# A 17-tap convolution by nested Toom-Cook products over groups of four batches

## The chip, the cores and the metric

The kernel runs on one core of a Trainium2 chip. The metric is the device time of that core in microseconds (us). A core has a matrix engine (TensorE, PE in the profile, its weight loads as PEld), three engines for elementwise work (VectorE or DVE, ScalarE or ACT, GpSimd or POOL) and a queue, SyncE or SP, that issues the DMA transfers. Each engine takes its own instructions in the order of the program and waits on the others by semaphores.

## The reference

For 32 batches of 512 tokens with 256 channels (B = 32, N = 512, D = 256), all in float32:

```python
h = jnp.maximum(_layernorm(x, axis=-1), 0.0)
xc = jnp.transpose(h, (0, 2, 1))
c = relu(bn1(conv1d(xc, conv1_w, pad=0)))                 # one tap
c = bn2(conv1d(c, conv2_w, pad=8))                        # 17 taps, 256 -> 256 channels
x_conv = jnp.transpose(relu(c + xc), (0, 2, 1))
s = h @ w_se.T + b_se                                     # three coordinates
A = jnp.exp(-squared_distance(s, s)) * adj
x_nmp = A @ relu(h @ w_msg.T + b_msg)
gi = jnp.concatenate([x_conv, x_nmp], axis=-1) @ w_ih.T + b_ih
gh = h @ w_hh.T + b_hh
r, z = sigmoid(gi_r + gh_r), sigmoid(gi_z + gh_z)
n = jnp.tanh(gi_n + r * gh_n)
out = x + (1 - z) * n + z * h
```

## The kernel before

One batch is worked after the other. Channels lie on the 128 partitions (two chunks of 128, ND = 2) and the 512 tokens on the free dimension; the layer norm, the messages and the residual have tokens on partitions (four chunks, NT = 4). Each output of 128 channels by 512 tokens fills one PSUM bank; there are five banks for sums (`ps_acc`) and three for transposes and positions (`ps_tr`). `matmul_sum` (L68) issues nearly all matrix multiplications, so its line holds many stages and they are told apart by the names of their tiles. A float32 multiplication is two MATMUL records in the trace, a float32 transpose is one.

The stages of a batch, each a function:
- `load`, `load_adj` (L75, L79): DMA of `x` (512 KB) and of the mask (1 MB).
- `norm` (L160 to L166): statistics on DVE, the power -1/2 on POOL (L119), scaling on DVE.
- `norm_t` (L177, L178): eight transposes, then ReLU on ACT gives `hT`.
- `conv1` (L185): the one-tap convolution; ACT writes it into `h1`, which has 8 zeros at both ends of the tokens.
- `positions` (L194 to L197): the two factors `left` and `right` of the distances.
- `messages` (L209, L210), `kernel_exp` (L218, L220), `masked` (L231, L232), `gather` (L253).
- `conv2` (L243, L246): for each half of the output channels one sum of 17 taps by two input chunks, 34 multiplications of 512 columns; a tap is a shifted slice of `h1`.
- `gates` (L276 to L298): three gates for each half of the channels, on TensorE, ACT, DVE and POOL.
- `finish` (L307 to L312): transposes back, residual, output DMA.

The program order is written out by hand (`manual_schedule`), so a buffer that is to be used again makes its next user wait. In that order batch b's `conv1`, `positions`, `messages` and `kernel_exp` come first, then `finish` of batch b - 1, `norm` of b + 1, the first half of `conv2`, `masked`, the second half of `conv2`, `norm_t` of b + 1, `gather` and `gates`. All weights of the 17 taps (`w2`) stay in SBUF.

## Time and profile before

| what | value |
|---|---|
| device time, median of 3 runs | 3608.95 us (3608.85 to 3609.02) |
| span of the profiled execution | 3607.8 us |
| granted TensorE clock, mean | 0.999 |
| TensorE busy | 3585.4 us |
| DVE, ACT, POOL busy | 506.7, 493.6, 281.3 us |
| `conv2` multiplications (`ps_acc<-h,w`) | 4352 records, 1878.8 us busy |
| DMA over the span | 76.00 MB, mean 21 GB/s |

The span runs from the first to the last instruction of one profiled execution; 1.15 us lie between it and the median of the runs. Busy time is the union of an engine's instructions; matrix multiplications are pipelined, so the price of one in a row of them is the distance between starts, not its own duration. In a group of the profile stand the line, the engine, the operation, output and inputs by tile name, shapes and count, then busy time, mean duration of one in ns, and the idle time of the engine just before them with what ended it. The chain that ended last goes back from the last instruction to whatever released it.

### The profile page before, as it was taken

How to read it: one execution, taken by the hardware profiler on the slowest of the kernel's cores; microseconds unless marked ns; L12 is line 12 of the kernel's file. 1: busy time of each engine (PE TensorE's matmuls, PEld its weight loads, DVE VectorE, ACT ScalarE, POOL GpSimd, SP SyncE). 2: the span in 40 equal slices, each digit the busy share in tenths (PEclk: the TensorE clock that was granted, in tenths of full speed). 3: DMA queues.
4: the chain of work that ended last, by engine and by line, in shares of the span. 5: the costliest groups of instructions: out<-in, count | busy, mean ns of one | idle time of the engine just before them, and what ended most of it. 6: DMA issues, size and time to landing. Idle time of an engine off the chain costs nothing.

```text
span 3607.8 us, 21656 instructions
## 1 busy us (share of the span) xinstructions
PE 3585.4 (99%) x9344; PEld 1678.9 (47%) x9344; DVE 506.7 (14%) x1006; ACT 493.6 (14%) x704; POOL 281.3 (8%) x241
## 2 busy tenths in 40 slices
PE   9999999999999999999999999999999999999998
PEld 4444444444444444444444444444444444444444
DVE  1111111111111101111011110111101111111111
ACT  1111011110111101111011110111111111111110
POOL 0000000000000000000000000000000000000000
PEclk9999999999999999999999999999999999999999
DMA  3000000000000000000000000000000000000000
GB/s 136 24 12 12 24 24 24 12 17 19 24 24 12 24 12 24 24 12 24 12 24 24 12 24 12 24 23 22 14 12 24 24 24 12 12 24 24 6 6 6
DMA packets 53858, 76.00 MB, mean 21 GB/s; under 512 B 3202, under 2 KB 36098, under 8 KB 53634
## 3 DMA queue, kind: packets, MB, share of 16 engines
q1 hardware_dynamic: 53762, 74.61, 6.3%
q8 instruction: 73, 1.20, 0.1%
q14 instruction: 23, 0.19, 0.0%
HBM read 57.83 MB, written 16.78 MB: 21 GB/s over the span
## 4 chain that ended last, share of the span: by engine, by line
PE 98%; DVE 1%; issue 0%; DMA 0%; POOL 0%; POOLq 0%; ACT 0%; ACTq 0%; DVEq 0%
PE ps_acc L68 91%; PE ps_acc L218 3%; PE ps_tr L68 2%; PE ps_tr L177 1%; PE ps_tr L307 1%; DVE at L232 1%; PE ps_tr L231 1%; DVE conv_t L243 0%; DMA x_sb<-in_x_dram 0%; DVE st L160 0%; POOLq L389 0%; POOL gate_t L296 0%; POOL gate_t L297 0%; POOL rstd L119 0%; DVE mv L161 0%
## 5 line engine op out<-in xcount | busy, mean ns | idle before, releaser
L68 PE MATMUL ps_acc<-h,w 128*128 128x512 f32 x4352 | 1878.8, 592 | 0.0
L68 PEld LDWEIGHTS ps_acc<-h,w 128*128 128x128 f32 x4352 | 817.9, 189 | 1015.2 <-issue 1015.2
L68 PE MATMUL ps_acc<-xnmp,wih 128*128 128x512 f32 x768 | 360.9, 592 | 0.0
L68 PE MATMUL ps_acc<-xconv,wih 128*128 128x512 f32 x768 | 360.9, 592 | 0.0
L68 PE MATMUL ps_acc<-hT,whh 128*128 128x512 f32 x768 | 350.5, 592 | 0.0
L296 POOL TENSOR_TENSOR gate_t<-hT,nn 128x512 f32<-128x512 f32 x64 | 80.9, 1264 | 2965.1 <-ACT nn L291 2965.1
L246 ACT ACTIVATE xconv<-conv_t,bn_shift 128x512 f32<-128x512 f32 x64 | 46.2, 721 | 1924.0 <-DVE conv_t L243 1924.0
L243 DVE SCALAR_TENSOR_TENSOR conv_t<-ps_acc,bn_scale,hT 128x512 f32<-128x512 f32 x64 | 48.1, 751 | 1651.6 <-PE ps_acc L68 1651.6
L68 PEld LDWEIGHTS ps_acc<-xconv,wih 128*128 128x128 f32 x768 | 145.9, 190 | 183.7 <-issue 183.7
L68 PEld LDWEIGHTS ps_acc<-xnmp,wih 128*128 128x128 f32 x768 | 145.9, 190 | 183.7 <-issue 183.7
L68 PEld LDWEIGHTS ps_acc<-hT,whh 128*128 128x128 f32 x768 | 145.9, 190 | 183.7 <-issue 183.7
L68 PE MATMUL ps_acc<-at,msg 128*128 128x512 f32 x512 | 225.0, 592 | 0.0
L68 PEld LDWEIGHTS ps_acc<-at,msg 128*128 128x128 f32 x512 | 94.9, 190 | 107.6 <-issue 107.6
L68 PE MATMUL ps_acc<-hT,w 128*128 128x512 f32 x256 | 117.1, 600 | 0.0
L279 DVE SCALAR_TENSOR_TENSOR gate_t<-ps_acc,vec,r 128x512 f32<-128x512 f32 x64 | 48.1, 751 | 484.8 <-ACT r L276 484.8
L68 PE MATMUL ps_acc<-wmsg,hT 128*128 128x256 f32 x512 | 115.7, 379 | 0.0
L218 PE MATMUL ps_acc<-right,left 67*128 67x512 f32 x256 | 115.1, 592 | 0.0
L68 PEld LDWEIGHTS ps_acc<-wmsg,hT 128*128 128x128 f32 x512 | 97.3, 190 | 28.5 <-issue 16.9
L289 DVE TENSOR_TENSOR gate_t<-ps_acc,gate_t 128x512 f32<-128x512 f32 x64 | 44.3, 692 | 411.6 <-PE ps_acc L68 411.6
L276 ACT ACT_TABLE_LOAD x32 | 41.1, 1283 | 377.5 <-PE ps_acc L68 377.5
L298 POOL TENSOR_TENSOR o_sb<-nn,gate_t 128x512 f32<-128x512 f32 x64 | 80.9, 1264 | 5.0
L297 POOL TENSOR_TENSOR gate_t<-z,gate_t 128x512 f32<-128x512 f32 x64 | 80.9, 1264 | 5.0
(52 smaller groups left out, 1261.5 us busy)
## 6 DMA issues: line engine op xcount, KB each, us to landing
m_sb<-in_adj_dram SPq DMA_DIRECT2D x32, 1024.0 KB, 5.3
x_sb<-in_x_dram SPq DMA_DIRECT2D x32, 512.0 KB, 4.0
out_dram<-y SPq DMA_DIRECT2D x64, 256.0 KB, 2.4
w<-in_conv_w_dram SPq DMA_DIRECT2D x4, 768.0 KB, 9.4
wih<-in_w_ih_dram SPq DMA_DIRECT2D x1, 1536.0 KB, 16.8
w<-in_conv_w_dram SPq DMA_DIRECT2D x2, 640.0 KB, 9.4
whh<-in_w_hh_dram SPq DMA_DIRECT2D x1, 768.0 KB, 15.1
w<-in_conv_w_dram SPq DMA_DIRECT2D x1, 256.0 KB, 3.5
```

The source lines that it names most:

```text
L68: nc.tensor.matmul(ps, lhsT, rhs, start=(i == 0), stop=(i == len(pairs) - 1))
L177: nc.tensor.transpose(ps[:, c * P : (c + 1) * P], xn[:, c, d * P : (d + 1) * P], ident)
L218: nc.tensor.matmul(ps, left[:, c * P : (c + 1) * P], right, start=True, stop=True)
L231: nc.tensor.transpose(ps[:, n * P : (n + 1) * P], m[:, n, c * P : (c + 1) * P], ident)
L243: nc.vector.scalar_tensor_tensor(t, ps, bn2_sc[:, o : o + 1], HT[b][:, o, :], op0=ALU.mult, op1=ALU.add)
L246: nc.scalar.activation(xconv[:, o, :], t, AF.Relu, bias=bn2_sh[:, o : o + 1])
L276: nc.scalar.activation(r, ps_r, AF.Sigmoid, bias=brz[:, o : o + 1])
L279: nc.vector.scalar_tensor_tensor(t, ps_h, vec[:, _COL["b_hh"] + 2 * ND + o : _COL["b_hh"] + 2 * ND + o + 1], r, op0=ALU.add, op1=ALU.mult,)
L289: nc.vector.tensor_tensor(t, ps_n, t, op=ALU.add)
L296: nc.gpsimd.tensor_tensor(t, hT[:, o, :], nn, op=ALU.subtract)
L297: nc.gpsimd.tensor_tensor(t, z, t, op=ALU.mult)
L298: nc.gpsimd.tensor_tensor(o_sb[:, o, :], nn, t, op=ALU.add)
```

## The change

The 17 taps are padded to 18 = 2 x 3 x 3. A level of the scheme takes three outputs and three taps at a time and makes five products of them (at the points 0, 1, -1, 2 and infinity); two nested levels give 25 products, each of the two taps that are left, for nine outputs. Four batches (G = 4) are worked together: a batch's 512 tokens are 57 blocks of nine (U = 57, 513 outputs), so each product is a sum of four multiplications of 4 x 57 = 228 columns for each half of the output channels.

- Operands: `fives` makes five combinations of the inputs on DVE, at the first level from `h1` (9 instructions of 1415 elements a partition, inputs three elements apart), at the second from each of the five results (9 of 471 each).
- Weights: `weights_first` combines the taps on DVE (`taps_of`), scales them on ACT, and stores the 25 sets of 512 KB to DRAM during the first group; later groups load them again (`weights_again`), two products ahead.
- Sums: `summed` takes the 25 products out of PSUM one by one (ACT copies, DVE adds) into `z` and `y`; after the fifth of each five come the larger additions. At the end of a group ACT spreads `y` into `xconv` with the batch norm, and DVE adds the channel-major rows, loaded again from DRAM into `hTb` (two buffers), batch after batch.
- Order: `convolution` issues a product's two halves; `rest` holds all stages of an earlier batch but the rows; `rows` makes `norm`, `norm_t` and `conv1` of the next group. The loop at the end draws from these generators in turn: each step of the other stages adds its stated time times `share` to `ahead`, each half product takes 1.65 off, and products are issued while `ahead` is above zero. A group begins at `ahead` = 0. The last four batches' `rest` comes after the last group.
- Buffers: PSUM has three banks for products, three for sums, two for transposes; `h1`, `left`, `right`, the mask and the messages have one buffer each; `norm` writes in place. `hT` is stored to DRAM (`HD`), and `x` is loaded a second time for the residual. Gates, messages and masked kernel compute the same as before, some in place.

The diff, cut to its core:

```diff
     _COL[_n] = _NCOL
     _NCOL += _w
+G = 4
+U = 57
+V = U + 2
+ROW = 9 * V
...
+ORDER = (3, 0, 4, 2, 1)
+GSCALE = (0.5, -0.5, -1.0 / 6.0, 1.0 / 6.0, 1.0)
...
-    io = ctx.enter_context(tc.tile_pool(name="io", bufs=2))
-    work = ctx.enter_context(tc.tile_pool(name="work", bufs=2))
-    one = ctx.enter_context(tc.tile_pool(name="one", bufs=1))
-    acc = ctx.enter_context(tc.tile_pool(name="acc", bufs=5, space=PSUM))
-    tr = ctx.enter_context(tc.tile_pool(name="tr", bufs=3, space=PSUM))
+    front = ctx.enter_context(tc.tile_pool(name="front", bufs=2))
+    cv = ctx.enter_context(tc.tile_pool(name="cv", bufs=1))
+    dram = ctx.enter_context(tc.tile_pool(name="dram", bufs=1, space=bass.MemoryType.DRAM))
+    cps = ctx.enter_context(tc.tile_pool(name="cps", bufs=3, space=PSUM))
+    acc = ctx.enter_context(tc.tile_pool(name="acc", bufs=3, space=PSUM))
+    tr = ctx.enter_context(tc.tile_pool(name="tr", bufs=2, space=PSUM))
...
+    def load_h(b):
+        HB[b] = late.tile([P, ND, N], F32, name="hTb", bufs=2)
+        nc.sync.dma_start(HB[b], HD[b])
...
+    prep = prep_ctx.enter_context(tc.tile_pool(name="prep", bufs=1))
+    wraw = prep.tile([P, ND, 2, 3, 3, D], F32)
+    nc.gpsimd.memset(wraw[:, :, 1, 2, 2, :], 0.0)
...
-    w2 = const.tile([P, ND, TAPS, D], F32)
-    for c in range(ND):
-        for k0, k1 in ((0, 6), (6, 12), (12, TAPS)):
-            nc.sync.dma_start(w2[:, c, k0:k1, :], conv2_w[:, c, k0:k1, :])
...
-    h1s = []
-    for i in range(2):
-        t = const.tile([P, ND, N + 2 * PAD], F32, name=f"h1_{i}")
...
+    h1 = const.tile([P, NR, ROW], F32)
...
+    left = const.tile([67, N], F32)
+    right = const.tile([67, N], F32)
...
+    HD = {b: dram.tile([P, ND, N], F32, name=f"hd{b}") for b in range(B)}
...
+            XS.pop(b)
+            nc.sync.dma_start(HD[b], HT[b])
...
+    def fives(get, new, n):
+        def sub(dst, a, b):
+            nc.vector.tensor_tensor(dst, get(a), get(b), op=ALU.subtract)
+        def less2(dst, a, b):
+            nc.vector.scalar_tensor_tensor(dst, a, -2.0, b, op0=ALU.mult, op1=ALU.add)
+        d1 = new()
+        sub(d1[:, :n], 3, 1)
+        yield d1
+        for a, b in ((2, 0), (4, 2)):
+            t = new()
+            sub(t[:, :n], a, b)
+            if b == 0:
+                less2(t[:, :n], t[:, :n], d1[:, :n])
+            else:
+                less2(t[:, :n], d1[:, :n], t[:, :n])
+            yield t
+        f2 = new()
+        sub(f2[:, :n], 3, 2)
+        t = new()
+        sub(t[:, :n], 2, 1)
+        less2(t[:, :n], t[:, :n], f2[:, :n])
+        yield t
+        less2(f2[:, :n], get(1), f2[:, :n])
+        yield f2
+    N1, N2 = NR * ROW // 3 - 1, NR * V - 1
+    def operands():
+        h1f = h1.rearrange("p r t -> p (r t)")
+        for x1 in fives(
+            lambda k: h1f[:, k : k + 3 * N1 - 2 : 3],
+            lambda: cv.tile([P, NR * ROW // 3], F32, name="x1", bufs=3),
+            N1,
+        ):
+            yield from fives(
+                lambda k: x1[:, k : k + 3 * N2 - 2 : 3],
+                lambda: cv.tile([P, NR * V], F32, name="x2", bufs=8),
+                N2,
             )
+    WD = [dram.tile([P, 2, ND, D], F32, name=f"wd{n}") for n in range(25)]
...
+    def weights_first():
...
+        for j1 in ORDER:
...
+                    nc.scalar.activation(
+                        w[:, :, i, :], next(inner[i]), AF.Copy, scale=GSCALE[j1] * GSCALE[j2]
+                    )
+                nc.sync.dma_start(WD[n], w)
+                n += 1
+                yield w
+    def weights_again():
+        for n in range(25):
+            w = cv.tile([P, 2, ND, D], F32, name="w", bufs=3)
+            nc.sync.dma_start(w, WD[n])
+            yield w
...
+    def summed(g):
+        y = cv.tile([P, 3, 3, NZ], F32, name="y")
+        for j1 in ORDER:
+            z = y[:, 0] if j1 == 3 else cv.tile([P, 3, NZ], F32, name="z")
+            ends = z[:, 0:3:2, :]
+            ps = yield
+            n3 = cv.tile([P, NZ], F32, name="n", bufs=3)
+            nc.scalar.activation(n3, ps, AF.Copy)
+            ps = yield
+            nc.vector.tensor_tensor(z[:, 0, :], ps, n3, op=ALU.add)
+            ps = yield
+            nc.vector.scalar_tensor_tensor(z[:, 2, :], n3, 4.0, ps, op0=ALU.mult, op1=ALU.add)
+            ps = yield
+            n2 = cv.tile([P, NZ], F32, name="n", bufs=3)
+            nc.scalar.activation(n2, ps, AF.Copy)
+            ps = yield
+            s = cv.tile([P, NZ], F32, name="s")
+            nc.vector.tensor_tensor(s, ps, n2, op=ALU.add)
+            nc.vector.tensor_tensor(n2, ps, n2, op=ALU.subtract)
+            nc.vector.tensor_tensor(ends, ends, s[:, None, :].to_broadcast([P, 2, NZ]), op=ALU.add)
+            nc.vector.scalar_tensor_tensor(z[:, 1, :], n3, 2.0, n2, op0=ALU.mult, op1=ALU.add)
+            zf = z.rearrange("p e n -> p (e n)")
+            yf = y.rearrange("p f e n -> p f (e n)")
+            if j1 == 3:
+                nc.scalar.activation(yf[:, 1], zf, AF.Copy, scale=2.0)
+                nc.scalar.activation(yf[:, 2], zf, AF.Copy, scale=4.0)
+            elif j1 == 0:
+                nc.vector.tensor_tensor(yf[:, 0], yf[:, 0], zf, op=ALU.add)
+            elif j1 == 4:
+                nc.vector.tensor_tensor(yf[:, 2], yf[:, 2], zf, op=ALU.add)
+            else:
+                ye = yf[:, 0:3:2, :]
+                nc.vector.tensor_tensor(
+                    ye, ye, zf[:, None, :].to_broadcast([P, 2, 3 * NZ]), op=ALU.add
+                )
+                nc.vector.tensor_tensor(
+                    yf[:, 1], yf[:, 1], zf, op=ALU.subtract if j1 == 2 else ALU.add
+                )
+        if late is None:
+            late_pools()
+        for b in range(g * G, (g + 1) * G):
+            load_h(b)
+            xc = XC[b] = late.tile([P, ND, 9 * U], F32, name="xconv", bufs=4)
+            for o in range(ND):
+                c = o * NU + b % G * U
+                nc.scalar.activation(
+                    xc[:, o, :].rearrange("p (u e f) -> p f e u", e=3, f=3), y[:, :, :, c : c + U],
+                    AF.Identity, bias=bn2_sh[:, o : o + 1], scale=bn2_sc[:, o : o + 1],
+                )
+            nc.vector.tensor_tensor(xc[:, :, :N], xc[:, :, :N], HB.pop(b), op=ALU.add)
+            nc.scalar.activation(xc[:, :, :N], xc[:, :, :N], AF.Relu)
+        yield
+    AHEAD, AHEAD_W = 4, 2
+    XC = {}
...
+        for g in range(NG):
...
+            for n in range(25):
+                while len(ws) < min(25 * g + n + 1 + AHEAD_W, 25 * NG):
+                    ws.append(next(wg))
+                while len(x2s) < min(25 * g + n + 1 + AHEAD, 25 * NG):
+                    if len(x2s) == 25 * (g + 1):
+                        yield "rows", g + 1
+                    x2s.append(next(xs))
+                    if len(x2s) == 25 * g + 21:
+                        yield "free", g
+                w, x2 = ws[25 * g + n], x2s[25 * g + n].rearrange("p (r v) -> p r v", v=V)
+                ps = cps.tile([P, NZ], F32, name="ps_c")
+                for o in range(ND):
+                    matmul_sum(
+                        ps[:, o * NU : (o + 1) * NU].rearrange("p (b u) -> p b u", u=U),
+                        [
+                            (w[:, k, i, o * P : (o + 1) * P], x2[:, i * G : (i + 1) * G, k : k + U])
+                            for k in range(2)
+                            for i in range(ND)
+                        ],
+                    )
+                    if o == 0 and done is not None:
+                        sums.send(done)
+                    yield "pe", 1.65
+                ws[25 * g + n] = x2s[25 * g + n] = None
+                done = ps
+            sums.send(done)
+            yield "group", g
...
+    def late_pools():
+        nonlocal late
+        prep_ctx.close()
+        late = ctx.enter_context(tc.tile_pool(name="late", bufs=1))
+        nc.sync.dma_start(whh, w_hh)
+        nc.sync.dma_start(wih, w_ih)
...
+            XR[b, c] = late.tile([P, 2, D], F32, name="y", bufs=3)
+            nc.sync.dma_start(XR[b, c], x[b].rearrange("(c p) d -> p c d", p=P)[:, c : c + 2, :])
...
+    def rest(b, following):
+        if b not in MS:
+            load_adj(b)
+        if b not in HB:
+            load_h(b)
...
+        positions(b)
+        yield 1.75
...
+            masked(b, at, c)
+            yield 0.55
+        MS.pop(b)
+        if following is not None:
+            load_adj(following)
+            load_h(following)
+        hT, xconv = HB.pop(b), XC.pop(b)
...
+    def rows(g):
+        bs = list(range(g * G, (g + 1) * G))
+        for b in bs[:2]:
+            if b not in XS:
+                load(b)
+            norm(b)
+        yield 0.0
+        for n, b in enumerate(bs + [None]):
+            if b is not None:
                 for d in range(ND):
-                    nc.tensor.transpose(
-                        ps[:, j, d * P : (d + 1) * P], o_sb[:, d, (c + j) * P : (c + j + 1) * P], ident
-                    )
-            y = io.tile([P, 2, D], F32, name="y")
-            nc.vector.tensor_tensor(y, ps, xs[:, c : c + 2, :], op=ALU.add)
-            nc.sync.dma_start(o_tok[:, c : c + 2, :], y)
-    norm(0)
+                    norm_t(b, d)
+                    yield 0.55
+            if n > 0:
+                for o in range(ND):
+                    conv1(bs[n - 1], o)
+                    yield 1.73
+            if n + 2 < G:
+                load(bs[n + 2])
+                norm(bs[n + 2])
...
+    def others(g):
+        bs = list(range((g - 1) * G, g * G)) if g > 0 else []
+        for b in bs[:-1]:
+            yield from rest(b, b + 1)
+        yield "rows wanted", g + 1
+        if g + 1 < NG:
+            yield from rows(g + 1)
+        yield "rows made", g + 1
+        for b in bs[-1:]:
+            yield from rest(b, None)
...
+        other = others(g)
+        share = 81.0 / (214.0 if 0 < g < NG - 1 else 196.0 if g else 18.0)
+        ahead = 0.0
...
+            if kind == "pe":
+                ahead -= value
...
+        while not ended:
+            if ahead > 0 or end:
+                step_conv()
+            else:
+                step_other()
+        while step_other():
+            pass
+    for b in range((NG - 1) * G, B):
+        for _ in rest(b, b + 1 if b + 1 < B else None):
+            pass
```

358 lines of the change are left out of this document (213 added, 145 removed).

## The prediction

> **What bounds the kernel now.** I read the page first, then the chain that ended last, then the stretches, and last the groups of instructions.
>
> ```profile
> span 3607.8 us, 21656 instructions
> PE 3585.4 (99%) x9344; PEld 1678.9 (47%) x9344; DVE 506.7 (14%) x1006; ACT 493.6 (14%) x704; POOL 281.3 (8%) x241
> ...
> PE 98%; DVE 1%; issue 0%; DMA 0%; POOL 0%; POOLq 0%; ACT 0%; ACTq 0%; DVEq 0%
> ```
>
> TensorE is busy 99% of the span, and 98% of the last chain is its own instructions: shorten its stream and the kernel gets shorter, until something else ends last. The full chain, in order of time, gives the price of a batch; a narrower window of it splits one batch:
>
> ```profile
> 86.42 41.20 PE ps_acc L68 x96
> ...
> 3447.63 41.20 PE ps_acc L68 x96
> ```
> ```profile
> 129.34 3.45 PE ps_acc L68 x16
> ...
> 137.10 29.21 PE ps_acc L68 x68
> ...
> 168.39 29.19 PE ps_acc L68 x68
> 197.59 0.87 PE ps_tr L177 x8
> ```
>
> The first two lines are the same place (gather and gates) of two batches 30 apart: 3361.21 / 30 = 112.04 us per batch. The second convolution of a batch is 29.21 + 29.19 = 58.40 us, so everything else is 53.64 us. A multiplication in float32 is two records here: 68 records of 512 columns in 29.21 us are 429.6 ns each, and 16 records of 256 columns (the messages) in 3.45 us are 215.6 ns each. That is 0.836 ns per column and 1.6 ns beside it.
>
> ```profile
> 0.00:24.00 24.00, 15.33 (x43) 8.64 (x44) 7.89 (x31) 7.69 (x11) 7.14 (x18) 1.00 0.81 287
> ...
> 86.42:198.46 112.04, 111.91 (x293) 52.40 (x293) 15.78 (x31) 15.41 (x23) 8.61 (x7) 1.00 0.06 19
> ...
> 3585.00:3607.80 22.80, 13.42 (x35) 6.24 (x34) 2.83 (x4) 2.10 (x3) 5.42 (x5) 0.87 0.07 23
> ```
>
> The columns are the stretch, then busy time and count for PE, weight loads, DVE, ACT and POOL, then granted clock and DMA. DVE and ACT work about 15 us of 112: there is room for about six times as much on each. The last stretch has clock 0.87, which I come back to.
>
> **Products instead of taps.** Removed: 2176 multiplications, 4352 records x 429.6 ns = 1869 us (58.40 x 32). Added: 8 groups x 25 products x 2 output halves x 4 multiplications = 1600, so 3200 records of 4 x 57 = 228 columns. The two prices above give 0.836 x 228 + 1.6 = 192.2 ns, 615 us in all or 76.9 us per group. The low end is the per-column share alone (191 ns, 611 us), the high end the 256-column price (215.6 ns, 690 us); I take 192, as the line through two rows. Weight loads could be what limits it:
>
> ```profile
> L68 PEld LDWEIGHTS ps_acc<-wmsg,hT 128*128 128x128 f32 x512 | 97.3, 190 | 28.5 <-issue 16.9
> ```
>
> A load takes 190 ns and hides behind the 215.6 ns multiplication before it; 192 ns would still just hide it. The TensorE sum is 32 x 53.64 + 615 = 1716.5 + 615 = 2331.5 us.
>
> **Work that moves to DVE and ACT.** No row has the new lengths, so I draw a line through two contiguous DVE shapes:
>
> ```profile
> L289 DVE TENSOR_TENSOR gate_t<-ps_acc,gate_t 128x512 f32<-128x512 f32 x64 | 44.3, 692 | 411.6 <-PE ps_acc L68 411.6
> L166 DVE TENSOR_SCALAR xn<-x_sb,mv,rstd 128x256 f32<-128x256 f32 x128 | 44.2, 409 | 36.3 <-POOL rstd L119 36.3
> L243 DVE SCALAR_TENSOR_TENSOR conv_t<-ps_acc,bn_scale,hT 128x512 f32<-128x512 f32 x64 | 48.1, 751 | 1651.6 <-PE ps_acc L68 1651.6
> L246 ACT ACTIVATE xconv<-conv_t,bn_shift 128x512 f32<-128x512 f32 x64 | 46.2, 721 | 1924.0 <-DVE conv_t L243 1924.0
> L291 ACT ACTIVATE nn<-gate_t,vec 128x512 f32<-128x512 f32 x64 | 46.2, 721 | 221.9 <-DVE gate_t L289 221.9
> L210 ACT ACTIVATE msg<-msg_t 128x512 f32<-128x512 f32 x64 | 40.3, 629 | 21.9 <-DVE msg_t L209 21.1
> L296 POOL TENSOR_TENSOR gate_t<-hT,nn 128x512 f32<-128x512 f32 x64 | 80.9, 1264 | 2965.1 <-ACT nn L291 2965.1
> L119 POOL TENSOR_TENSOR rstd<-veps,mhalf 128x4 f32<-128x4 f32 x32 | 32.6, 1017 | 342.6 <-DVE veps L118 342.6
> L160 DVE BATCH_NORM_STATS2 st<-x_sb 128x6 f32<-128x256 f32 x128 | 51.2, 400 | 12.7 <-DMA x_sb<-in_x_dram 12.7
> L161 DVE BATCH_NORM_AGGREGATE mv<-st 128x2 f32<-128x6 f32 x128 | 23.3, 182 | 4.4
> ```
>
> (692 - 409) / 256 = 1.105 ns per element and 0.126 us beside it, an estimate. Operands per group: 9 instructions of 1415 elements (1.69 us) and 45 of 471 (0.646 us), 44.3 us. Sums per group: five times five of 456 elements (0.63) and one of 912 (1.13), 21.4 us; then two of 1368 (1.64) and two pairs of 2736 and 1368 (3.15 + 1.64), 12.9 us. Adding the residual is 4 x 1.26 us, 5 us. With 4 x 14.3 us of the old work (15.8 less the two 0.75 us that leave with the convolution) DVE has 44.3 + 34.3 + 5 + 57 = 141 us per group, against 76.9 + 4 x 53.64 = 291.5 us of TensorE. ACT gains about 20 us per group. So TensorE still bounds the steady part, and the question is where it waits in its own order. TensorE, DVE, ACT and SP each run their queue in program order, and the generators fix that order. I went through it step by step.
>
> **The first group.** Nothing but the next group's rows lies beside it, and the products' weights are made on DVE: 10 instructions of 1536 (1.82) and 50 of 512 (0.692), 52.8 us. Operands 44.3, the next group's first five operands 1.69 + 9 x 0.646 = 7.5, sums 34.3, and four norms of 4.9 us (four stats and aggregates 2.3, the POOL power 1.0, four scalings 1.6) 19.6: together 158.5 us of DVE for 76.9 us of products.
>
> ```profile
> 4.55 0.43 DVE L160 BATCH_NORM_STATS2 st<-x_sb 128x6 f32<-128x256 f32 x1 [3.46 <-DMA x_sb<-in_x_dram]
> ...
> 10.80 5.58 PE L68 MATMUL ps_acc<-hT,w 128*128 128x512 f32 x8
> ```
> ```profile
> 124.02 3.60 PE L68 MATMUL ps_acc<-hT,w 128*128 128x512 f32 x8
> ```
>
> The first norm starts at 4.55 us now. After the change the affine constants come first (3 us) and then four norms of 4.9 us: DVE is free for weights at about 31.5 us. The third and fourth batch load behind 4.46 MB of taps, at the 287 GB/s of the first stretch 15.5 us, so by 21.5 us, in time. The first group's sums end at 31.5 + 158.5 = 190 us. TensorE has by then done 76.9 us of products and eight batches of rows (eight transposes 0.87 and eight conv1 records 3.44, 4.31 us each, 34.5 us): 78 us idle. Low end 45 (neighbouring DVE instructions overlap), high end 115.
>
> **The end of each group.** After a group's last gate matmul (time 0) the program has: DVE add (0.2 + 0.69), the last sums (four of 0.63, 1.13, 3.15, 1.64), done at 8.7 us. Then per batch, in turn because ACT keeps its order: two Identity of 0.72, the residual add 1.26, a Relu of 1024 elements (at most 2 x 0.629; I take 1.2) and three hand-offs of about 0.05 (my estimate), 4.05 us. Ahead of all this lies the next group's first instruction for TensorE: `positions` of a batch whose channel-major rows are loaded anew. The group's end uses both `hTb` buffers for the same rows, batch after batch, so this fifth load waits for the third residual add, at 8.7 + 8.1 + 2.8 = 19.6 us, and lands 4.0 us later:
>
> ```profile
> x_sb<-in_x_dram SPq DMA_DIRECT2D x32, 512.0 KB, 4.0
> ```
>
> TensorE stands for 23.6 us: at a group's start nothing has been counted ahead, so the other stages go first and the products that could run lie behind `positions`. Such a pause also costs clock. The eight conv1 records took 5.58 us at the cold start and 3.60 us later, and after the one pause at the end seven transposes took 1.75 us:
>
> ```profile
> 3602.20 1.75 PE L307 MATMUL ps_tr<-ident,o_sb 128*128 128x128 f32 x7 [5.53 <-POOL o_sb L298]
> ```
>
> I add 2.0 us. The first group's end has the sums in its 190 us already: 16.9. In all 7 x 25.6 + 16.9 = 196 us. If the loads could be had early this would be 0; if the scattered ACT writes cost double, 20 us more.
>
> **What I cost at nothing.** From the second group on each product's weights come back from memory, 512 KB on SP's queue, which takes 4.0 us for as much `x` (the row above) and has two products of about 13 us each for it. Such a load waits until TensorE has left the third buffer, and behind it on SP stand mask, row and output transfers. They come out at most one product late, and each is issued a product or more before its use, but for `hTb` above; without that cover a late mask would cost up to 5 us per batch. ACT's 20 us lie beside TensorE.
>
> **Rows in the middle of a group.** `norm_t` needs a norm that stands behind the last gate's add on DVE and behind its three POOL instructions (3 x 1.26 from about 1.65 us, when add and tanh are done, then the power 1.0, then four scalings): 7.9 us, while TensorE has one half product, 1.5 us: 6.4 us. The second norm ends 4.9 us later against 0.9 us of transposes: 3.6 us more. The third and fourth are covered by conv1 and half products. 10 us in six groups: 60 us, from 20 to 90.
>
> **Sums that stand in front of other stages.** Every fifth product puts 7.8 us on DVE at once. Mostly gates of 5.2 us cover it. In the fourth batch it falls after the first `kernel_exp`: the two finish adds start at 9.2 us, TensorE wants the transpose buffer at 7.4 and then waits on adds of 0.69 through two `ps_tr` buffers: about 3.3 us; in the other batches about 1 us each. 8 us x 7 groups = 56 us, from 0 to 140. The last four batches run with no products between: six DVE instructions of 0.69 there against 24 transposes of 0.11, and exps that free three `ps_acc` buffers: 3.5 us each, 14 us.
>
> **The sum.** After the last gate the present kernel takes
>
> ```profile
> 3596.60 0.69 DVE L289 TENSOR_TENSOR gate_t<-ps_acc,gate_t 128x512 f32<-128x512 f32 x1 [6.98 <-PE ps_acc L68]
> ```
>
> 3607.8 - 3596.6 = 11.2 us to the span's end, and 1.15 us lie between the span and the median of the runs (3608.95). So 2331.5 + 78 + 196 + 60 + 56 + 14 + 11.2 + 1.15 = 2748 us. A measurement of this kernel can tell 0.2% from no change.
>
> **The rivals.**
> First, the group ends are covered, because the loads or residual adds come out earlier than my order has them. For it: DMA is at 6% in a batch. Against it: TensorE keeps its order. 2748 - 196 = 2552 us. Chance 0.15.
>
> Second, operands with a step cost more. Six of nine operand instructions read every third word. No instruction of the present kernel reads so; bounds are one and two times the contiguous rate. At two times: 29.5 us more per group; the first group 34 us longer, group ends 2.6 us each by ACT's scattered writes (21 us), the stalls inside groups double (56): 2748 + 111 = 2859 us. Chance 0.19. [...]
>
> Third, the weight load is not hidden at 228 columns: 190 + 192 ns in series, 607 us more, 3355 us. Against it is the row at 256 columns. Chance 0.03.
>
> Fourth, slower: the many small waits keep TensorE's clock down. With 415 us of waits, work of 2331.5 (1 + f) passes 3609 from f = 0.37, a mean granted clock under 0.73; at half clock throughout it is 5080 us. For it: the 0.87 of the last stretch. Against it: only the group ends and the rows pause for 5 us. Chance 0.03. [...]
>
> **How the numbers follow.** The forecast has 0.60, its own range 2640 to 2850 (products 611 to 690, first group, rows and sums by their ends, not all at once). With the first two rivals the range is 2540 to 2880. Faster: 0.60 + 0.15 + 0.19 + 0.03 = 0.97; same 0.01 and slower 0.02 share the fourth.
>
> **What would show it.** Right: 3200 records of 228 columns at 192 ns apart; DVE about 1180 us busy (459 + 8 x 83.6 + 53) and still under half; eight TensorE pauses of 17 to 24 us in front of `positions`, put down to the `hTb` load; a period of about 335 us per group; first `positions` near 205 us. Wrong: no such pauses (first rival); operand instructions of 1415 elements well over 1.7 us (second); records over 215 ns apart (third); a granted clock well under 0.9 in the middle (fourth).

## The result and the profile after

The changed kernel takes 2827.52 us, the median of four runs (2824.37 to 2832.12); the kernel before takes 3608.90 in the runs beside them. The ratio is 0.7836, 95% interval 0.7825 to 0.7847: 781 us less. The forecast of 2748 us was 80 us too low; the range held the time. Times are medians of the fast executions of a kernel, which leaves out a single slow one, of 9123.65 us, in the run on the spread without a step. The profiled execution took 2832.12 us, of which 2830.3 are its span. Its page, first lines and chain:

```profile
span 2830.3 us, 20941 instructions
PE 2429.8 (86%) x8192; PEld 1498.6 (53%) x8192; DVE 1233.2 (44%) x1750; ACT 651.2 (23%) x882; POOL 310.0 (11%) x240
...
PE 77%; DVE 14%; ACT 4%; issue 3%; DMA 2%; POOL 1%; POOLq 0%; SPq 0%; DVEq 0%; ACTq 0%
```

TensorE was 99% of the span and 98% of the chain; now it is 86% and 77%. DVE is busy for only 44% of the span and yet is 14% of the chain: it has room on the average, and TensorE waits for it at certain places. The stretches (length, busy time and count of PE, weight loads, DVE, ACT and POOL, granted clock, DMA share, GB/s) show where: the start, the first group, the next two groups and the last four batches:

```profile
0.00:47.90 47.90, 23.09 (x64) 11.92 (x65) 28.12 (x73) 15.19 (x23) 8.80 (x20) 0.96 0.55 207
47.90:195.40 147.50, 110.07 (x464) 92.76 (x464) 130.02 (x193) 43.07 (x72) 4.03 (x4) 0.86 0.31 117
195.40:547.80 352.40, 307.17 (x1018) 189.28 (x1016) 149.12 (x210) 75.84 (x102) 37.26 (x25) 0.92 0.27 94
547.80:891.80 344.00, 301.30 (x1026) 186.38 (x1024) 147.48 (x210) 77.93 (x104) 37.00 (x28) 0.94 0.26 87
2581.60:2830.30 248.70, 204.42 (x570) 98.84 (x568) 61.07 (x77) 60.22 (x77) 37.99 (x27) 0.93 0.15 51
```

In the first group DVE is busy for 130.0 of 147.5 us: there it is the bound. A later group takes 344 us, of which TensorE works 301 and DVE 147. The clock is 0.92 to 0.94 in every one of them. What TensorE waited for (total, times, longest):

```profile
PE ps_tr L86 <- DMA hTb<-hd: 200.2, 7, 29.7
PE ps_tr L195 <- DVE x_sb L184: 68.5, 9, 14.6
PE ps_tr L452 <- DVE y L468: 28.2, 29, 7.0
PE ps_tr L86 <- issue: 27.4, 1, 27.4
```

The first and the last line are eight pauses in front of `positions`, as forecast, but of 28 us and not of 17 to 24. The second is the transposes of the next group's rows, waiting for their norm (14.6 us of it are the start of the kernel). One group's end in order of time (start, duration, engine, line, output and inputs, in brackets the idle time before):

```profile
1228.70 1.70 PE L86 MATMUL ps_c<-x,w 128*128 128x228 f32 x8
1230.24 1.88 PE L86 MATMUL ps_acc<-xconv,wih 128*128 128x512 f32 x4
...
1233.88 0.69 DVE L545 TENSOR_TENSOR r<-ps_acc,r 128x512 f32<-128x512 f32 x1 [8.04 <-PE ps_acc L86]
...
1235.46 1.27 POOL L552 TENSOR_TENSOR gate_t<-hTb,r 128x512 f32<-128x512 f32 x1 [17.28 <-ACT r L546]
1235.69 2.01 DVE L331 TENSOR_TENSOR z<-z,s 128x912 f32<-128x912 f32 x1
...
1236.81 2.01 POOL L553 TENSOR_TENSOR gate_t<-z,gate_t 128x512 f32<-128x512 f32 x1
1237.62 1.69 DVE L332 SCALAR_TENSOR_TENSOR z<-n 128x456 f32<-128x456 f32 x1
1238.89 1.53 POOL L554 TENSOR_TENSOR o_sb<-r,gate_t 128x512 f32<-128x512 f32 x1
1239.34 3.95 DVE L344 TENSOR_TENSOR y<-y,z 128x2736 f32<-128x2736 f32 x1
...
1244.82 2.35 ACT L357 ACTIVATE xconv<-y,bn_shift,bn_scale 128x513 f32<-128x513 f32 x2 [9.50 <-DVE y L347]
...
1253.42 0.43 SPq L97 DMA_DIRECT2D m_sb<-in_adj_dram  x1
...
1257.64 0.32 SPq L101 DMA_DIRECT2D hTb<-hd  x1
...
1263.50 3.68 PE L86 MATMUL ps_tr<-hTb,wse 128*67 128x512 f32 x4 [29.66 <-DMA hTb<-hd]
```

Eight product records start 1230.24 - 1228.70 = 1.54 us before what follows them: 192.5 ns each, the forecast's 192. After the last gate's add (1233.88) the sums end when ACT begins to spread `y` (1244.82), 10.94 us later; three cycles of spread, add and ReLU then free the buffer (12.82 us); the load is issued at 1257.64 and `positions` starts at 1263.50 (5.86 us).

For the accounts below I priced every TensorE record by the full-clock distances of the prediction (429.6, 215.6 and 192.2 ns, transposes 110), called the excess of a record that lies in a stretch of half clock a clock loss, and the rest of the excess a wait. That gives 2322.7 us of work, 67.6 us of clock loss and 420 us of waits; with 14.6 us before the first record and 5.4 after the last start they make the span.

### The profile page after: what moved, and what is told of

The parts are those of the page before. It is cut to its first block, busy times and chain, and to the rows that moved or that the text cites. A ratio compares the mean times of both kernels' runs of the same rounds, so it can differ in the third digit from the quotient of the medians.

```text
span 2830.3 us, 20941 instructions
## 1 busy us (share of the span) xinstructions
PE 2429.8 (86%) x8192; PEld 1498.6 (53%) x8192; DVE 1233.2 (44%) x1750; ACT 651.2 (23%) x882; POOL 310.0 (11%) x240
## 3 DMA queue, kind: packets, MB, share of 16 engines
q1 hardware_dynamic: 113506, 246.60, 25.4%
## 4 chain that ended last, share of the span: by engine, by line
PE 77%; DVE 14%; ACT 4%; issue 3%; DMA 2%; POOL 1%; POOLq 0%; SPq 0%; DVEq 0%; ACTq 0%
PE ps_acc L86 49%; PE ps_c L86 18%; PE ps_tr L452 3%; PE ps_acc L444 3%; PE ps_tr L86 2%; DVE x L217 2%; ACT xconv L357 2%; PE ps_tr L195 2%; DVE x L220 1%; DMA hTb<-hd 1%; DVE xconv L361 1%; DVE y L347 1%; DVE z L331 1%; DVE y L468 1%; ACT xconv L362 1%
## 5 line engine op out<-in xcount | busy, mean ns | idle before, releaser
L86 PEld LDWEIGHTS ps_c<-x,w 128*128 128x128 f32 x3200 | 620.7, 195 | 182.1 <-issue 150.1
L86 PE MATMUL ps_c<-x,w 128*128 128x228 f32 x3200 | 694.4, 363 | 24.2 <-DVE z L321 8.2
L86 PE MATMUL ps_acc<-hTb,whh 128*128 128x512 f32 x768 | 361.8, 596 | 0.0
L552 POOL TENSOR_TENSOR gate_t<-hTb,r 128x512 f32<-128x512 f32 x64 | 92.4, 1444 | 2276.4 <-ACT r L546 1510.2
L86 PE MATMUL ps_tr<-hTb,wse 128*67 128x512 f32 x128 | 74.3, 711 | 227.6 <-DMA hTb<-hd 200.2
L533 DVE SCALAR_TENSOR_TENSOR r<-ps_acc,vec,r 128x512 f32<-128x512 f32 x64 | 48.1, 751 | 449.9 <-ACT r L531 449.9
L86 PEld LDWEIGHTS ps_acc<-hTb,whh 128*128 128x128 f32 x768 | 145.2, 192 | 115.3 <-issue 114.5
L220 DVE SCALAR_TENSOR_TENSOR x<-x,x 128x471 f32<-128x471 f32 (+1 forms) x184 | 158.5, 861 | 5.3
L217 DVE TENSOR_TENSOR x<-x 128x471 f32<-128x471 f32 x200 | 157.7, 807 | 1.4
L195 PE MATMUL ps_tr<-ident,x_sb 128*128 128x128 f32 x256 | 56.3, 365 | 89.8 <-DVE x_sb L184 68.5
```

Of the source, the lines that this page charges most:

```text
L86: nc.tensor.matmul(ps, lhsT, rhs, start=(i == 0), stop=(i == len(pairs) - 1))
L195: nc.tensor.transpose(ps[:, c * P : (c + 1) * P], xn[:, c, d * P : (d + 1) * P], ident)
L217: nc.vector.tensor_tensor(dst, get(a), get(b), op=ALU.subtract)
L220: nc.vector.scalar_tensor_tensor(dst, a, -2.0, b, op0=ALU.mult, op1=ALU.add)
L533: nc.vector.scalar_tensor_tensor(r, ps_h, vec[:, _COL["b_hh"] + 2 * ND + o : _COL["b_hh"] + 2 * ND + o + 1], r, op0=ALU.add, op1=ALU.mult,)
L552: nc.gpsimd.tensor_tensor(t, hT[:, o, :], r, op=ALU.subtract)
```

## The experiments

Each starts from the changed kernel unless it says otherwise. The theory: what is missing lies in front of `positions` at the group ends, in TensorE's own order. The main rival: the work of the group end itself must be waited for, wherever the pause is put.

**Products first.** A group starts eight half products ahead of the other stages:

```diff
-        share = 81.0 / (214.0 if 0 < g < NG - 1 else 196.0 if g else 18.0)
-        ahead = 0.0
+        first = 13.2 if g else 0.0
+        share = (81.0 - first) / (214.0 if 0 < g < NG - 1 else 196.0 if g else 18.0)
+        ahead = first
```

> Four products (eight half products, 12.3 us) are issued at the head of each group from the second on, before `positions`; the share of the other stages is lowered so that a group still ends the same way. My theory (TensorE stands in its own order behind a `positions` whose rows load late): the 28.6 us pause in front of `positions` shrinks by the 12.3 us at seven group starts, 86 us in all, to about 2740 us; the eighth, with no products left, stays. Rival (the pause is the time that sums and residual need, whoever goes first): products only move, the pause stays near 28 us, no change beyond 10 us.

It took 2824.7 us: no change, and my expectation missed. TensorE now paused before the third product, whose weights are loaded again; TensorE's order of time, then SP's:

```profile
1244.38 5.40 PE L86 MATMUL ps_c<-x,w 128*128 128x228 f32 x16 [18.16 <-DMA w<-wd]
```
```profile
1234.69 4.91 SPq L101 DMA_DIRECT2D hTb<-hd  x2
1239.69 10.44 SPq L308 DMA_DIRECT2D w<-wd  x4
```

SP issued in order: the `w` loads begin at 1239.69, 0.09 us after the two `hTb` loads in front of them (1234.69 + 4.91). The weights stand behind the `hTb` loads that wait for the residual adds, so the wait came back in SP's queue. The prediction counted such loads as covered; that holds only while products do not stand ahead of the group end.

**Own buffers for the residual's rows.** With them, `positions` need not wait for the group end's buffers:

```diff
-            load_h(b)
+            hr = late.tile([P, ND, N], F32, name="hTr", bufs=2)
+            nc.sync.dma_start(hr, HD[b])
...
-            nc.vector.tensor_tensor(xc[:, :, :N], xc[:, :, :N], HB.pop(b), op=ALU.add)
+            nc.vector.tensor_tensor(xc[:, :, :N], xc[:, :, :N], hr, op=ALU.add)
...
-            yield from rest(b, None)
+            yield from rest(b, b + 1)
```

> The residual additions at a group's end read their rows from two buffers of their own, and the next group's first batch has its rows and mask loaded during the last batch's gates. Rival (the late hTb load is the whole cause): the pause of 28.6 us goes, 8 x 28.6 = 229 us, to about 2600 us. My theory (DVE and ACT order stands behind it): `positions` runs at once, but `left` waits on DVE behind the sums and four residual additions, so a pause of about 22 us appears in front of `kernel_exp` instead; 8 x 7 = about 55 us faster, about 2770 us.

It took 2814.1 us, 13 less, where the eight pauses hold 229. The wait has another name:

```profile
PE ps_acc L445 <- ACT left L430: 167.9, 9, 26.2
```

`left` is made on DVE and ACT, behind the residual adds and the spread. Waits fell by 41 us, and clock loss rose by 26 (from 67.6 to 93.9). The mechanism was mine, the gain less than a third of what I gave it.

**Residual later.** The residual add and the ReLU of a batch move from the group end into its own `rest`, after `masked`, where its rows are at hand anyway:

```diff
-            load_h(b)
...
-            nc.vector.tensor_tensor(xc[:, :, :N], xc[:, :, :N], HB.pop(b), op=ALU.add)
-            nc.scalar.activation(xc[:, :, :N], xc[:, :, :N], AF.Relu)
...
         hT, xconv = HB.pop(b), XC.pop(b)
+        nc.vector.tensor_tensor(xconv[:, :, :N], xconv[:, :, :N], hT, op=ALU.add)
+        nc.scalar.activation(xconv[:, :, :N], xconv[:, :, :N], AF.Relu)
```

> The residual addition and its Relu move from the group's end into each batch's own stages, after the masked kernel, where the batch's rows are there anyway; the eight spreading Identity instructions stay at the group's end, back to back. My theory: `positions` starts about 4 us after the last gate, then `kernel_exp` waits for `left` and `right` behind eight Identity of 1.17 us that start at 11 us, so about 10 us more; 14 instead of 28.6 us, 8 x 14.6 = 117 us, about 2710 us. Rival (the hTb load alone): 8 x 24 = 190 us, about 2635 us.

It took 2732.1 us, 95 less: 22 above my forecast and 97 above the rival's, so the late load was not the whole cause. What is left in front of `kernel_exp` is the spread on ACT and the sums on DVE:

```profile
PE ps_acc L441 <- ACT left L426: 98.5, 9, 15.9
```

**The spread later too.** Besides the edit before, the eight Identity instructions of a group end wait until the next group has begun, and the last batch of a group loads the next group's first rows:

```diff
-        for b in range(g * G, (g + 1) * G):
...
+        spread.append((g, y))
...
+        if b not in XC:
+            spread_out()
         while waiting:
...
-            yield from rest(b, None)
+            yield from rest(b, b + 1)
```

> Edit: the group ends alone. The spread of y into xconv waits until the next group has begun, the residual add and ReLU of a batch stand behind its own masked kernel, and the last batch of a group loads the rows of the next group's first batch; the norms and the order of products stay. My theory: the fifth load no longer waits for anything, so the eight pauses in front of positions (229 us) go; VectorE still has the last sums of the group (11.1 us after the gate) in front of left, against 5.2 us of positions and messages: 7 x 6 = 45 us in front of kernel_exp, with some 10 us more half clock: 2620 to 2670 us, near 2640. Rival: the spread in its new place (ten us on ScalarE) makes the sums and the exponentials late, and half or more of the 229 us stays in front of kernel_exp: 2710 us or more.

It took 2679.0 us, 149 less than the changed kernel, and 9 us over my bounds. The waits came out as expected (242.6 us, of them 60 in front of `kernel_exp`); clock loss rose from 67.6 to 94.6 us, by 27 where I had 10. (This run was made after the combined versions below, to see the deferral alone.) One such place, in the order of time and then as a stretch:

```profile
1190.51 7.20 PE L450 MATMUL ps_acc<-right,left 67*128 67x512 f32 x8 [5.54 <-ACT left L435]
```
```profile
1188.40:1202.10 13.70, 11.59 (x24) 6.97 (x24) 7.33 (x8) 9.94 (x14) 0.00 (x0) 0.50 0.00 1
```

After a pause of 5.5 us TensorE works 11.6 us at clock 0.50: I count 5.7 us lost in this stretch. The long pause of the changed kernel also has a long stretch of half clock, but TensorE hardly works in it (shown further down).

**TensorE kept busy in the pause.** 30 multiplications of constants, whose sum is overwritten, stand in front of each group's first `positions`:

```diff
         ps = tr.tile([P, N], F32, name="ps_tr")
+        if b % G == 0:
+            for _ in range(30):
+                nc.tensor.matmul(ps, ident, zero, start=True, stop=True)
```

> Thirty extra multiplications of a constant by the identity (60 records, 25.8 us) run in front of `positions` of each group's first batch, inside the 28.6 us pause, into a bank that is overwritten. The load of the rows comes no earlier, so whatever the time loses is clock. My theory: 67.6 us are lost to half clock in all, of which the group ends have 2 to 3 us each: 16 to 24 us faster, 2804 to 2812 us, and the granted clock rises from 0.93 to about 0.98. Rival (the low clock after a pause costs nothing because later waits take it up): no change within 6 us.

It took 2821.6 us, 6 less; the rival's bound was met, mine was not. The pauses are filled,

```profile
PE ps_tr L86 <- DMA hTb<-hd: 20.4, 7, 3.6
```

and the stretches of half clock halve from 392.5 to 193.3 us, but clock loss only falls from 67.6 to 61.4. So the clock at the group ends is a small matter; the loss lies behind the shorter pauses.

**The norms early.** The norms of the next group's first two batches move in front of the group's third `rest`:

```diff
         for b in bs[:-1]:
+            if b == bs[2] and g + 1 < NG:
+                norms(g + 1)
             yield from rest(b, b + 1)
```

> Edit: the norms of the next group's first two batches stand in front of the group's third rest, not behind its last gates; nothing else. My theory: the pauses in front of the next group's first transposes (6.19 + 2.80 us in each of six groups, 54 us in all in the changed kernel's trace) come from these norms standing on DVE and POOL behind the gates, and each costs 2 to 3 us of half clock as well: about 54 + 14 = 68 us less, near 2760 us, and the waits put down to x_sb nearly gone. Rival: the transposes then wait for something else at the same place (the gates' own additions and the sums keep DVE late): less than 20 us gained, over 2807 us, with the wait under another name. A second rival: the norms in their new place delay that batch's masked kernel, and the gain comes back as waits on m_sb or right, left: 2780 to 2810 us.

It took 2868.4 us, 41 more. My theory missed; the second rival had the mechanism at too small a price, the first a number without its mechanism. The waits of the transposes fell by 30 us, but those in front of `kernel_exp` rose by 48, and clock loss by 18:

```profile
1074.27 1.38 DVE L184 TENSOR_SCALAR x_sb<-x_sb,mv,rstd 128x256 f32<-128x256 f32 x4 [3.52 <-POOL rstd L143]
...
1080.41 0.73 DVE L426 TENSOR_SCALAR left<-ps_tr,bse 3x512 f32<-3x512 f32 x1
...
1083.32 2.92 PE L444 MATMUL ps_acc<-right,left 67*128 67x512 f32 x3 [7.39 <-ACT left L429]
```

The two norms, some 12 us with their two waits for POOL, stand right in front of `left`, which TensorE needs at once.

**Operands without a step.** The operand instructions read neighbouring elements (this computes products of other numbers, and the output is not the convolution):

```diff
-            lambda k: h1f[:, k : k + 3 * N1 - 2 : 3],
+            lambda k: h1f[:, k : k + N1],
...
-                lambda k: x1[:, k : k + 3 * N2 - 2 : 3],
+                lambda k: x1[:, k : k + N2],
```

> Edit: the operand instructions of both levels read neighbouring elements in place of every third (same count, same lengths; the products are then of other numbers, so what is computed is not the convolution). My theory: the step costs a factor of 1.24 (2127 against 1713 ns at 1415 elements), about 7 us of DVE per group; DVE is the limit only in the first group (7 us, some 2 more for the next group's first operands) and is hidden in the others: 10 to 25 us less, 2802 to 2818 us, and L217 at 1.7 us for 1415 elements. Rival (the second rival of the prediction, stepped operands as what keeps the kernel from its forecast): the stalls inside the groups are made by the long operand instructions: 55 us less or more, under 2772 us.

It took 2805.0 us, 22.5 less, within my bounds. The rows (minimum, median and maximum duration in ns) of the changed kernel, then of this one:

```profile
L217 DVE TENSOR_TENSOR x<-h x40: 2065/2099/3184, 44.9 to 2424.3; 128x1415 f32<-128x1415 f32 x40
```
```profile
L217 DVE TENSOR_TENSOR x<-h x40: 1621/1624/2698, 45.1 to 2397.9; 128x1415 f32<-128x1415 f32 x40
```

By the medians the step costs 2099 / 1624 = 1.29 at 1415 elements (1.24, 795 against 640 ns, at 471), and not 2 as the second rival had it; my 1.24 came from comparing two kinds of instruction.

**The spread without a step.** The Identity writes one element behind the other in place of nine apart (the tokens come out in another order, and the output is not the reference's):

```diff
-                    xc[:, o, :].rearrange("p (u e f) -> p f e u", e=3, f=3), y[:, :, :, c : c + U],
+                    xc[:, o, :].rearrange("p (f e u) -> p f e u", e=3, f=3), y[:, :, :, c : c + U],
```

> Edit: the spread of y into xconv writes its elements one behind the other in place of nine apart (same count; the tokens of the convolution's output come out in another order, so what is computed is not the convolution). My theory: the scattered write makes an Identity 1268 ns in place of about 0.72, two of them stand in each of the three cycles ahead of the fifth load, 3 x 2 x 0.5 = 3 us per group end: 24 us less, near 2803 us, with each positions pause near 26 us. Rival: the Identity costs what it does because of its scattered read (57 of 228 elements at a time) or its other work, not the write: no change, within 6 us of 2827, L357 still near 1.27 us.

It took 2804.6 us (median of three), 22.9 less. Changed kernel first, then this one:

```profile
L357 ACT ACTIVATE xconv<-y,bn_shift,bn_scale x64: 1247/1268/1298, 204.4 to 2608.1; 128x513 f32<-128x513 f32 x64
```
```profile
L357 ACT ACTIVATE xconv<-y,bn_shift,bn_scale x64: 799/801/816, 204.3 to 2581.5; 128x513 f32<-128x513 f32 x64
```

467 ns less for each of six in a group end, eight times, are 22.4 us: the scattered write is the cause, and it lies on the path in full.

**The gates' GpSimd work on DVE.**

```diff
-            nc.gpsimd.tensor_tensor(t, hT[:, o, :], r, op=ALU.subtract)
-            nc.gpsimd.tensor_tensor(t, z, t, op=ALU.mult)
-            nc.gpsimd.tensor_tensor(o_sb[:, o, :], r, t, op=ALU.add)
+            nc.vector.tensor_tensor(t, hT[:, o, :], r, op=ALU.subtract)
+            nc.vector.tensor_tensor(t, z, t, op=ALU.mult)
+            nc.vector.tensor_tensor(o_sb[:, o, :], r, t, op=ALU.add)
```

> Edit: the three GpSimd instructions of the gates run on VectorE, in the same order and with the same numbers. My theory: the group-end sums (L331 2.01, L332 1.69, L344 3.95 us at the second end) are long because VectorE with two SBUF inputs and GpSimd run at the same time; without GpSimd they take 1.10, 0.63 and 3.01 us as at the first group's end. That gains 2.9 us per end and loses about as much, since VectorE has the tanh to wait for and three additions of 0.7 us first: 2815 to 2840 us. Rival: they are long for another reason (the sums wait for ScalarE's copies, or TensorE's traffic): durations as they are now, and 8 x 2.9 us or more lost: 2845 us or more.

The long additions are gone. Changed kernel first, then this one:

```profile
L331 DVE TENSOR_TENSOR z<-z,s x32: 1098/1098/2007, 93.3 to 2584.0; 128x912 f32<-128x912 f32 x32
...
L344 DVE TENSOR_TENSOR y<-y,z x16: 3007/3009/3952, 178.4 to 2586.7; 128x2736 f32<-128x2736 f32 x16
```
```profile
L331 DVE TENSOR_TENSOR z<-z,s x32: 1097/1098/1101, 91.3 to 2597.8; 128x912 f32<-128x912 f32 x32
...
L344 DVE TENSOR_TENSOR y<-y,z x16: 3007/3009/3010, 176.6 to 2599.5; 128x2736 f32<-128x2736 f32 x16
```

So the mechanism of my theory holds: the longest L331 takes 1.10 us in place of 2.01, the longest L344 3.01 in place of 3.95. The time, 2851.7 us, fell in the rival's bounds all the same: 24 us more. The gate's instructions on DVE take back what the sums gain, and the pauses in front of `positions` stay at 229.8 us; the norms behind them come later, and the transposes wait 11 us more, `kernel_exp` 4 us. (The profiled execution, 2845.4 us, is 13 above that of the changed kernel, and this accounts for it; what made the other three runs longer, 2851 to 2859 us, no profile shows.)

**All of it.** The deferred spread, now after `kernel_exp` with `z` in two buffers of its own, four half products ahead, and the early norms:

```diff
-        y = cv.tile([P, 3, 3, NZ], F32, name="y")
+        y = None
...
-            z = y[:, 0] if j1 == 3 else cv.tile([P, 3, NZ], F32, name="z")
+            z = cv.tile([P, 3, NZ], F32, name="z", bufs=2)
...
+                nc.scalar.activation(yf[:, 0], zf, AF.Copy)
...
+        first = 6.6 if g else 0.0
...
+            if b == bs[2] and g + 1 < NG:
+                norms(g + 1)
```

> Edit: all that the earlier runs point to, with the same computation: the spread of y stands behind the next group's kernel_exp, the residual add and ReLU of a batch behind its own masked kernel, each rest loads the next batch's rows early (the next group's first too), the norms of the next group's first two batches stand early, and a group starts four half products ahead. My theory: the group ends' 229 us, the rows' 54 us and most of 40 us of half clock behind them go, and some 20 us come back as waits on the sums and the spread: 2480 to 2560 us, near 2515. Rival: the pause is the DVE and ACT work of the group end itself, and TensorE meets it wherever it is put (as when the rows had their own buffers, which gave 13 of 160 us): 2640 us or more.

It took 2711.1 us, 32 more than the deferred spread alone. It is 151 us above my upper bound; the rival's number held, not its reason:

```profile
PE ps_tr L86 <- DMA hTb<-hd: 7.0, 1, 7.0
...
PE ps_acc L452 <- ACT left L437: 80.5, 13, 8.6
```

The group ends are gone but for the first. `left` is late thirteen times: six times it stands on DVE behind early norms (7.4 us each), six times behind the next group's first operands (4.6 us each) and once behind a fifth product's sums (8.6 us). Those sums also make `msg` late six times, 18.8 us in all.

**Positions early.** If that is so, `positions` has to be issued before that work. On the kernel before this one: `positions` of the next batch stands in front of the last gate, a norm at a time in the first gates of the second and third batch, `conv1` right behind its own transposes, six half products ahead:

```diff
-        positions(b)
+        if b not in POS:
+            positions(b)
...
+            if o == 0 and early is not None:
+                norm(early)
...
+            if o == ND - 1 and following is not None:
+                positions(following)
+                POS.add(following)
             ps_n = acc.tile([P, N], F32, name="ps_acc")
```

> Edit, on the version with covered group ends: positions of the next batch stands in front of the last gate of the batch before; the norms of the next group's first two batches stand singly in the gates of its second and third batch; each conv1 follows its own transposes; a group starts six half products ahead. The computation is the same. My theory: what was left (112 us in front of kernel_exp, 66 in front of the next group's transposes, 109 us of half clock, most of it right behind these) is work that TensorE needs at once and that stands on VectorE behind longer work; put earlier, 90 + 40 us of waits and 50 us of half clock go: 2500 to 2580 us, near 2525, with the wait on left under 25 us. Rival: VectorE's sums delay the next thing in line instead (the additions of the messages, and by them the banks of kernel_exp): the same pauses under another name, 2650 us or more.

It took 2555.1 us (2552.8 to 2557.6), ratio to the kernel before 0.7080 (0.7069 to 0.7091): 272 us under the changed kernel. Page, waits and one group:

```profile
PE 2404.9 (94%) x8192; PEld 1486.4 (58%) x8192; DVE 1210.5 (47%) x1750; ACT 653.6 (26%) x890; POOL 295.8 (12%) x240
```
```profile
PE ps_acc L452 <- DVE msg L447: 31.5, 7, 7.3
PE ps_tr L195 <- DVE x_sb L184: 26.7, 2, 13.6
```
```profile
520.70:827.90 307.20, 299.39 (x1024) 185.79 (x1024) 143.88 (x209) 78.07 (x105) 36.61 (x28) 0.98 0.28 91
```

A group takes 307.2 us for 291.5 us of work; the waits for `left` are gone, clock loss is 48 us. My theory held, the rival did not: DVE is busy for nearly as long (1210.5 us, 1233.2 in the changed kernel), and what changed is its order against TensorE's. The main rival of this section falls with it. How much each of the four moves gave was not tried apart.

**More products beside.** On that version, eight half products ahead in place of six, and half products drawn between `finish` and `masked`:

```diff
-        first = 9.9 if g else 0.0
+        first = 13.2 if g else 0.0
...
-            yield 0.87
+            yield 0.0
...
-                yield 0.55
+                yield 0.0 if c == 0 else 4.4
...
-            yield 0.55
+            yield 2.38 if c == 1 else 0.0
```

> Edit, on the version with early positions: a group starts eight half products ahead in place of six, and the steps in which half products are drawn are put between finish and masked and in the middle of masked. My theory: the 4.2 us pause in front of the second kernel_exp at each group start (31.5 us on the additions of the messages, and 17.8 us of half clock behind it) is VectorE still at the last sums, and two more half products cover it; half of the 33 us on the two transpose buffers goes too: 2480 to 2520 us, near 2500. Rival: the fourth product then waits for a product bank whose sum stands behind the same VectorE work, as when products were put first in the changed kernel: within 10 us of 2555.

It took 2577.8 us, 23 more. Both forecasts missed. The waits in `masked` fell from 50 to 31 us as meant, but four `kernel_exp` in a row, with no half product between, now wait for ACT (6.0 us before, 19.6 now):

```profile
PE ps_acc L452 <- ACT at L453: 19.6, 21, 1.4
```

Which of the two edits costs what was not tried apart.

## Why the prediction was right, and where its sizes failed

Its terms against the account of the changed kernel, in us. As in the prediction, the first 9.0 us of the first pause (from 195.3, where TensorE stops, to the end of the sums at 204.3) count with the first group. A clock loss stands with the pause that its stretch of half clock follows:

| term | predicted | measured |
|---|---|---|
| TensorE's work | 2331.5 | 2322.7 |
| first group, from the start to the end of its sums | 78 | 93.0 (14.6 start, 65.7 waits, 12.7 clock) |
| eight group ends | 196 | 237.2 (220.3 waits, 16.9 clock) |
| rows, six groups | 60 | 74.6 (57.9 waits, 16.7 clock) |
| sums ahead of other stages, last rests | 70 | 92.0 (70.6 waits, 21.4 clock) |
| end of the span, and around it | 12.4 | 12.8 |
| sum | 2748 | 2832.3 |

**Right.** The price of a product (192.2 ns), the weight load hidden behind it (189 ns in the median), DVE as the bound of the first group alone (busy 130.0 of 147.5 us), the place and the cause of the group-end pauses, and the waits inside groups within 3 us. For the sums, luck has a part in that: the prediction's own terms give 3.3 + 3 x 1 = 6.3 us a group and not its 8, and two groups in the middle of the run waited 7.4. DVE was busy for 1233 us and not for about 1180. The runs agree: the pause could be moved along the order of DVE, ACT and SP (three runs), and went away only when the work was put elsewhere.

**The term that failed: the group ends, 41 us.** Seven of them were put at 23.6 us and waited 28.8 on average. In the one shown, the sums took 10.94 us and not 8.7, the three cycles 12.82 and not 10.9, the load 5.86 and not 4.0. The sums are longer because DVE and GpSimd get in each other's way here. At the first group's end, where GpSimd is idle, DVE's order of time shows the same two instructions as

```profile
198.15 1.10 DVE L331 TENSOR_TENSOR z<-z,s 128x912 f32<-128x912 f32 x1
...
199.82 3.01 DVE L344 TENSOR_TENSOR y<-y,z 128x2736 f32<-128x2736 f32 x1
202.75 1.58 DVE L347 TENSOR_TENSOR y<-y,z 128x1368 f32<-128x1368 f32 x1
```

against 2.01 and 3.95 us above, and the run without GpSimd's gates showed it as the cause (there no L331 took over 1.10 us and no L344 over 3.01). In the group end shown, L331 starts 0.23 us after L552 and ends 0.91 us late; L553 starts inside L331 and takes 2.01 us where L552 took 1.27. Why the two hinder each other no run shows. The cycles are longer by the Identity, 1268 ns where a contiguous row had promised 721; without the scattered write it takes 801. The load takes 4.2 to 5.9 us in the eight ends. Each time it is issued 4.2 us behind the next batch's mask (1 MB), which lands 6.3 to 6.8 us after its own issue where the trace has the landing; loads of the same size that stand earlier in a group end, with no transfer beside them, land after 3.1 to 3.4 us. So the mask is the likely cause, but no run took it away. The first end, from 204.3 to `positions` at 223.0, took 18.7 us, where the prediction had 14.9 (and 2.0 of clock).

**The first group, 15 us.** Its sums end at 204.3 us and not at 190. DVE began the weights at 35.2 us and not at 31.5 (for which the prediction's own terms, 4.55 + 3 + 4 x 4.9, give only 27.2): its first norm started at 10.6 us, and the third waited for its `x` until 25.4 us, which the prediction had by 21.5. From there it needed 169.1 us and not 158.5. I had it busy without a gap but for POOL's 4 us; it was busy for 151.3, and its named waits were 5.4 us for rows, 4.8 for POOL, 3.1 for a product and 1.4 for ACT.

**The term that was missing: the clock behind short pauses, 38 us.** The prediction charged 2.0 us to each group end, which is about what was found (16.9 / 8 = 2.1), and nothing to the rows and the stalls in the groups, where 16.7 and 21.4 us went. A long pause spends most of its half clock with TensorE idle; of the stretches below, in the changed kernel, the first is a group end, the second follows 2.0 us of waiting for DVE; the row in the order of time where that wait ends is shown after it:

```profile
1239.50:1266.90 27.40, 3.40 (x4) 1.11 (x5) 10.19 (x6) 13.30 (x12) 0.93 (x1) 0.50 0.34 115
...
839.00:842.40 3.40, 3.40 (x13) 2.42 (x13) 2.53 (x4) 0.00 (x0) 0.00 (x0) 0.50 0.91 295
```
```profile
838.25 3.59 PE L452 MATMUL ps_tr<-ident,m_sb 128*128 128x128 f32 x16 [2.01 <-DVE y L468]
```

These 27.4 us of half clock hold 3.4 us of work (the whole stretch, 30.7 us, holds 5.6 and loses 2.7); the 3.4 us after the short wait are all work, and lose 1.7 us. The fourth rival counted the pauses of 5 us alone; here a wait of 2.0 us was followed by the same drop, to a clock of 0.50, as the 29.7 us of the group end. What fits this trace is the share of a window of 3.41 us in which TensorE is busy: before the drop at 839.0 us it was 0.41, before 30 of the 31 drops at most 0.49 (before the other 0.72), and no window at full clock without a drop behind it had less than 0.51.

**The rivals.** The first (group ends covered, 2552 us) did not happen in this order; that the version with `positions` early takes 2555 us with the same products is nearly its number, reached by other savings and with other waits left. The second (operands at twice the time, an assumption of mine) is refuted at 1.29, worth 22.5 us in all; its forecast of 2859 us was nearer to 2827 than mine of 2748, by a mechanism that is not there in that size. The weight load stayed hidden (189 ns, beside records 192.5 ns apart), and the clock never came near the break-even of the fourth: 0.931 on the mean.

## What to carry to other kernels

When the bounding engine's work shrinks, ask of each instruction it issues who makes its input and what stands ahead of that on the maker's queue: DVE was busy 44% and cost 14% of the chain, and the same work in another order gave 272 us. A wait that was removed at one place turned up here at the next instruction whose maker stood behind the same work (200.2 us at `positions`, then 167.9 us at `left` with the residual's own buffers; 18.2 us at the weights on SP in the group end with products first), so trace the whole of that work before pricing the gain. Price a short pause with the clock that follows it, not only with its length: behind the 2.0 us of waiting above, half clock lost 1.7 us more.

## What the hardware showed that was not expected

- The stretches of half clock add up to 392.5 us in 31 pieces whose lengths are multiples of 3.41 us (3.41, 6.83, 10.24, 27.3, 30.7). In the version with `positions` early, too, the clock falls behind windows of 3.41 us in which TensorE is busy for less than about half: at most 0.43 of the window before each of its 18 drops, at least 0.47 where it stayed full. Other runs hold a few exceptions (with the early norms a drop behind 0.73, and a window of 0.41 without one). Taking the long pauses away raised the clock loss with the spread deferred: 94.6 us, against 67.6 in the changed kernel.
- Reading float32 three elements apart costs DVE 1.29 times the contiguous time (2099 against 1624 ns); writing float32 nine elements apart costs ACT 1.58 times (1268 against 801 ns).
